# The first keys of attention issued beside the end of a feed-forward layer, in a float32 macaron block

## The chip, the cores and the metric

The kernel runs on one core of a Trainium2 chip, in float32. The number that counts is the device time of one execution in microseconds (us), as the median of several runs. The core has five engines that run side by side, each with its own queue in order: PE (matrix products; PEld is its weight load), DVE (vector), ACT (scalar functions), POOL (general, and here the issuer of the indirect gathers) and SP (issues most DMAs). An instruction waits in its queue until the data, or the memory, that it needs is free, and all that stands behind it on that engine waits as well.

## What is computed

Four batches of 512 positions with 512 features go through a feed-forward layer, an attention layer and the same feed-forward layer again, each with a layer norm ahead and a residual around it:

```
x = x + 0.5 * ffn(layernorm(x))
x = x + attention(layernorm(x))
x = x + 0.5 * ffn(layernorm(x))
```

The feed-forward layer has 2048 inner features. Its three weight matrices are read off cubic splines with few control points:

```
inter = silu(x @ gate_w.T) * (x @ up_w.T)
return inter @ down_w.T
```

The attention is a gated delta rule. Of 16 heads each has one query, one key and two values of 128 features; they pass a causal convolution of four taps and a silu:

```
q = rms_norm(q); k = rms_norm(k)
beta = sigmoid(b_gate); g = -exp(A_log) * softplus(a_gate + dt_bias)
S = S * exp(g_t)
delta = (v_t - k_t @ S) * beta_t
S = S + outer(k_t, delta)
o = q_t @ S
```

The outputs are normalised, multiplied by silu(z) and brought back to 512 features.

## The kernel before

**Program.** `ffn(x -> x1, build=True)`, `attention(x1 -> x2)` and `ffn(x2 -> out, build=False)` run one after the other. x1 and x2 are DRAM tiles, one for each batch. On-chip memory and PSUM are handed out by pools on a stack: a pool that is opened after another was closed gets the same addresses, so its first writes wait until the last users of the old tiles are done.

**Feed-forward layer** (L297). The first call (FFN1) builds its weights from the splines during the first batch (`spline_weights`, L632); pw (L412) is a small constant that is set to zero by DVE. `hidden` makes pg and pu for 16 blocks of 128 inner features (L434), ACT takes silu, DVE multiplies (L443), SP writes the block to DRAM (`hid`, L444). `gather` brings the 2048 rows back in another order, 16 indirect DMAs on POOL (L453). `project` multiplies them by the down weights: sums pm (L477) with copies fm, blocks y<-wr (L487), the rest y<-we (L490) and y<-cm (L493). `back` copies y to yg (L499), transposes it (y_pt, L504) and adds it, in 44 small pieces called boxes, to a copy of x (`ffn_xr`, L532); then the batch is stored (L510). `turn_of(b)` interleaves by hand the hidden products of batch b+1 with the projection of batch b and the `back` of batch b-1; what is left over runs at its end, all gathers first, then units of work one after the other. The last batches have no hidden products to lie beside. In this stage the order on all five engines is the order written, SP's among them.

**Attention** (L798). Work is cut in 64 units, (batch, head). The opening loads constants (cst, cw, wba, dtb, nega, nwh), sets `ones`, two `tt` tiles and `nn` to their constants by POOL (L820, L870), then does for batch 0 the layer norm (`begin(0)`: xt loaded at L883, statistics L888, pow on POOL L893, subtraction and product L895, transposes ln_pt L902), the gates (pb L909, then DVE and ACT), sums of decays (pgs, pe: L969, L978), and **eight keys ahead** (LEAD). A key is: load of w_k (L1049, one buffer), four steps of pj<-xnT,w_k (L998, eight matmul records), taps of the convolution (L1006 on ACT, three L1008 on DVE), tanh (L1016), k (L1020), then its 32x32 blocks pkk (L1029), dg, squares and weights (L1034 to L1088), scan and product dd (L1095, L1098). After four keys `invert` works on their blocks (L1109 to L1128) in many short DVE instructions. Then slots: `slot(un)` prepares unit un (q, v; taps again), makes the key of unit un+8, runs the recurrence of un-1 and the output of un-2. The opening and the slots are in an order written by hand on PE, DVE, ACT and POOL, with SP left to the scheduler. Attention's tiles in PSUM: pa has four banks, shared by ln_pt, pb, pgs, pe, pj and pkk in the opening; pi and pq have two each.

**Feed-forward layer again.** The second call (FFN2) loads its weights from DRAM, loads batch 0 (`ffn_x`, L328), takes statistics (L336 to L341), normalises (ln_xn, L356), transposes (ln_pt, L363) and starts with pf (L369).

Of the kernel before, what the change touches and what calls it, by code (L numbers as in the profile page):

```python
# [1 line left out]

# [15 lines left out]
P = 128  # L18
# [244 lines left out]
def tile_macaron(ctx, tc, x, w_qkvz, w_ba, conv_w, dt_bias, a_log, norm_w, w_out, cps, consts, grid, starts, out):  # L263
# [32 lines left out]

    def ffn(src, dst, build):  # L297
        with ExitStack() as st:
            wp = st.enter_context(tc.tile_pool(name="ffn_w", bufs=1))
            io = st.enter_context(tc.tile_pool(name="ffn_io", bufs=2))  # L300
            fp = st.enter_context(tc.tile_pool(name="ffn_feat", bufs=2 * NG_F))
            sm = st.enter_context(tc.tile_pool(name="ffn_sm", bufs=2))
            wk = st.enter_context(tc.tile_pool(name="ffn_wk", bufs=2))
            ps = st.enter_context(tc.tile_pool(name="ffn_ps", bufs=2, space=PSUM))
            py = st.enter_context(tc.tile_pool(name="ffn_py", bufs=1, space=PSUM))

# [10 lines left out]
            def tick():  # L317
                clock[0] += 1
                for f in calendar.pop(clock[0], ()):
                    f()  # L320

            def drain():
                while calendar:
                    tick()
# [77 lines left out]
            else:  # L402
                for g in range(NG_F):
                    nc.sync.dma_start(wc[g].rearrange("p m i -> p (m i)"), wg_d[g])
                ft = whole(xt)
            wdp = st.enter_context(tc.tile_pool(name="ffn_wd", bufs=1))
            wr = wdp.tile([P, NB, P], F32, name="wr")
# [8 lines left out]
            if not build:  # L416
                nc.sync.dma_start(wr.rearrange("p c h -> p (c h)"), wr_d)
                nc.sync.dma_start(we, we_d)
                nc.sync.dma_start(cm.rearrange("p c h -> p (c h)"), cm_d)
            ip = st.enter_context(tc.tile_pool(name="ffn_inter", bufs=2))  # L420

            def hidden(b, ft):

                to, box = hid[b % 2], {}

                def gate(k):
                    if build and b == 0:
                        block(k, wr, we, cm)
                    product(k, 0)

                def product(k, m):
                    at = (k % 2) * P
                    pm = box[m] = ps.tile([P, S], F32, name=("pg", "pu")[m], tag="gu")
                    nc.tensor.matmul(pm, wc[k // 2][:, m, at : at + P], ft[k // 2], start=True, stop=True)  # L434
                    if m:
                        pg = box[0]
                        later(1, lambda: finish(k, pg, pm))

                def finish(k, pg, pu):
                    sg = wk.tile([P, S], F32, name="ffn_sg")  # L440
                    nc.scalar.activation(sg, pg, AF.Silu)
                    it = ip.tile([P, S], F32, name="ffn_it", bufs=4)
                    nc.vector.tensor_tensor(it, pu, sg, ALU.mult)  # L443
                    nc.sync.dma_start(to[k * P : (k + 1) * P, :], it)  # L444

                return [f for k in range(NB) for f in (lambda k=k: gate(k), lambda k=k: product(k, 1))]
# [14 lines left out]
            def project(b, nat):  # L461
# [35 lines left out]
                def evict(g):  # L497
                    yg = box["yg", g] = wk.tile([P, S], F32, name="yg", tag="yg", bufs=4)
                    nc.scalar.copy(yg, box["y"][g])  # L499
# [44 lines left out]
            def turn_of(b):  # L544
# [10 lines left out]
                plan["nat"], steps = gather(b + 1)  # L555
                tail, early = plan["tail"], []
                for i in range(4):
                    early += [*tail[i : i + 1], *turns[i : i + 1]]
                early += inter
                lead = 6 * 2 if b >= 0 else len(main)  # L560
                for i, f in enumerate(main):
# [9 lines left out]
                    tick()  # L571
                    n = -(-len(early) // max(1, lead - i)) if i < lead else 0
                    if i >= 2 or not turns:
                        for f in early[:n]:
                            f()
                            tick()
                        early = early[n:]
                    if i >= lead:
# [5 lines left out]
                        units = units[n:]  # L584
                drain()

                for f in steps if b + 1 < B else ():
                    f()
                for f in early + units:
                    f()  # L590
                    tick()
                plan["tail"] = back

            by_hand = lambda: tc.manual_schedule(
                engines={e.engine for e in (nc.tensor, nc.vector, nc.scalar, nc.gpsimd, nc.sync)}
            )
# [4 lines left out]
            if build:  # L601
# [16 lines left out]
                built.close()  # L618
            np_ = st.enter_context(tc.tile_pool(name="ffn_nat", bufs=NB + 4))
            with by_hand():  # L620
                if build:
                    plan["nat"], steps = gather(0)
                    for f in steps:
                        f()
                for b in range(0 if build else -1, B):
                    turn_of(b)
                for f in plan["tail"]:
                    f()
                    tick()
                drain()  # L630

    def spline_weights(st, scratch, wc, ps):  # L632

        sp = st.enter_context(tc.tile_pool(name="spl", bufs=1, side="right"))
        s2 = st.enter_context(tc.tile_pool(name="spl2", bufs=2, side="right"))
        c1 = scratch.enter_context(tc.tile_pool(name="spl_c1", bufs=1))
# [158 lines left out]

    def attention():  # L798
        with ExitStack() as st:
            pool = lambda name, bufs, **k: st.enter_context(tc.tile_pool(name=name, bufs=bufs, **k))  # L800
            ac = pool("at_c", 1)
            sm = pool("at_sm", 2)
            sn = pool("at_sn", LEAD + 3)
            w1 = pool("at_w1", 1)
            w2 = pool("at_w2", 2)
            w3 = pool("at_w3", 3)
            w4 = pool("at_w4", 4)
            wkeys = pool("at_k", LEAD + 2)
            pa = pool("at_pa", 4, space=PSUM)
            pi = pool("at_pi", 2, space=PSUM)  # L810
            pq = pool("at_pq", 2, space=PSUM)

            def bank(p, name, shape):
                return p.tile(shape, F32, name=name, tag="bank")

# [3 lines left out]
            ones = ac.tile([P, P], F32, name="ones")  # L819
            nc.gpsimd.memset(ones, 1.0)  # L820
            gt = cst[:, C_GT : C_GT + P]
# [35 lines left out]
            def due():  # L857
                for f in calendar.pop(clock[0], ()):
                    f()
# [9 lines left out]
            for x_ in (*tts, nn):  # L869
                nc.gpsimd.memset(x_, 0.0)  # L870

# [170 lines left out]
            def keys(b, n, bt, s, dd, slot):  # L1042

                xnT, beta, g, eg, neg = (bt[k] for k in ("xnT", "beta", "g", "eg", "neg"))
                at = n * 6 * DK + DK
# [30 lines left out]
                def weights(ms, rs):  # L1076
# [4 lines left out]
                    w = sn.tile([P, NT, 2], F32, name="w")  # L1081
                    nc.vector.tensor_tensor(w, beta[:, :, n, :], bc(rk2, 2, 2), ALU.mult)
                    nw = sm.tile([P, NT, 2], F32, name="nw")
# [510 lines left out]

            with tc.manual_schedule(engines={e.engine for e in (nc.tensor, nc.vector, nc.scalar, nc.gpsimd)}):
                batches[0], load, turn_x, raw, sums = begin(0)
                for t in range(NT):
                    load(t)
                    drain()
                    turn_x(t)  # L1600
                for f in (raw, sums):
                    f()
                    drain()
                made, first = [], iter(())
                ahead = min(LEAD, N)
                for un in range(ahead):
                    if un == GRP:
                        drain()
                        first = invert(diag[0], inverse[0])
                    made.append(keys_of(un))  # L1610
                    made[un]["load"]()
                    made[un]["decay"]()
                    for f in made[un]["dense"]:
                        f()
                        clock[0] += 1
                        due()
                        for _ in range(2):
                            next(first, None)
                    later(6, made[un]["blocks"])
                    if un in (GRP - 1, ahead - 1):  # L1620
                        drain()
                if ahead == GRP:
                    first = invert(diag[0], inverse[0])
                for _ in first:
                    pass
                for un in range(N + 2):
                    slot(un)
                drain()

    ffn(lambda b: x[b], lambda b: x1[b], True)  # L1630
    attention()
    ffn(lambda b: x2[b], lambda b: out[b], False)


# [30 lines left out]
```

## Time and profile before

The time is 3882.93 us, the median of 3 runs (3880.99 to 3885.04). The profiled execution:

| | |
|---|---|
| time of the profiled execution | 3887.16 us |
| its span (first to last instruction) | 3885.4 us |
| PE busy | 3594.6 us (93%) |
| DVE busy | 2631.4 us (68%) |
| ACT busy | 1463.3 us (38%) |
| POOL busy | 855.7 us (22%) |
| mean granted clock of PE | 0.965 |
| last hidden product of FFN1 (pu, L434) | 342.72 us |
| last transposes y_pt of FFN1 | 402.05 to 403.96 us |
| last py product of attention | ends at 3540 us |

Times in lines of the profile are in us from the start of the span. A line of the timeline gives start, duration, engine, source line, operation, output<-input, shape and count, and in square brackets the idle time of the engine just before and what ended it. "SPq" rows are the issue of DMAs, not their flight. A row of windows gives for one stretch of time each engine's busy time and count, then the granted clock of PE, the DMA engines' busy share and GB/s. In the view of 40 slices each digit is a busy share in tenths.

The stages: FFN1 up to 409 us, attention's opening from there to 551, slots to 3540, FFN2 to the end.

### The profile page before, as it was taken

The numbers are of one execution on the slowest core, as the hardware profiler recorded it, in microseconds if no ns is written. First come the engines' busy times: TensorE is split into PE (matmuls) and PEld (weight loads), VectorE is DVE, ScalarE is ACT, GpSimd is POOL, SyncE is SP. The second block draws the span as 40 slices with busy tenths as digits, with TensorE's granted clock in tenths as the row PEclk, the third lists the DMA queues.
The fourth block names the chain that finished last, engine by engine and source line by source line (L and its number), as shares of the span: only waits on it lengthen the run. The fifth ranks groups of instructions, "written<-read, shape, count | busy, mean of one in ns | idle before, by whom it ended". The sixth has DMA issues, their size and how long they took to land. (4 is left out here: it accounts for less than half of the span.)

```text
span 3885.4 us, 62488 instructions
## 1 busy us (share of the span) xinstructions
PE 3594.6 (93%) x24568; PEld 1975.0 (51%) x24568; DVE 2631.4 (68%) x5927; ACT 1463.3 (38%) x3432; POOL 855.7 (22%) x662
## 2 busy tenths in 40 slices
PE   5998569999999999999999999999999999987998
PEld 2332235555555555555555555555555555553333
DVE  5232387788788878878877887888888777652321
ACT  2221113444444444344444443444444444442221
POOL 2113022222222222222222222222222222120221
PEclk7999679999999999999999999999999999997999
DMA  4435211222222222221222221122122211112452
GB/s 140 149 129 174 84 40 57 68 65 58 63 58 63 60 79 61 64 61 58 63 70 80 61 73 54 58 64 59 58 79 64 71 50 55 50 36 95 150 192 98
DMA packets 303093, 302.25 MB, mean 78 GB/s; under 512 B 96880, under 2 KB 231312, under 8 KB 302224
## 3 DMA queue, kind: packets, MB, share of 16 engines
q1 hardware_dynamic: 292560, 264.70, 21.9%
q0 software_dynamic: 10240, 33.56, 2.8%
q8 instruction: 194, 3.18, 0.3%
q14 instruction: 99, 0.81, 0.1%
HBM read 247.60 MB, written 50.59 MB: 77 GB/s over the span
## 5 line engine op out<-in xcount | busy, mean ns | idle before, releaser
L1008 DVE SCALAR_TENSOR_TENSOR acc<-pj,cw,acc 128x511 f32<-128x511 f32 (+2 forms) x768 | 573.7, 747 | 150.1 <-ACT acc L1006 132.0
L998 PE MATMUL pj<-xnT,w_v 128*128 128x512 f32 x1024 | 521.1, 602 | 0.0
L1461 PE MATMUL py<-w_o,gT 128*128 128x512 f32 x1024 | 514.8, 616 | 0.4
L1313 PE MATMUL pz<-w_z,xnT 128*128 128x512 f32 x1024 | 514.5, 614 | 0.0
L443 DVE TENSOR_TENSOR ffn_it<-pu,ffn_sg 128x512 f32<-128x512 f32 x128 | 88.4, 691 | 363.6 <-PE pu L434 253.4
L998 PE MATMUL pj<-xnT,w_k 128*128 128x512 f32 x512 | 267.3, 631 | 19.5 <-DMA w_k<-in_L_attn_W_qkvz 19.5
L998 PE MATMUL pj<-xnT,w_q 128*128 128x512 f32 x512 | 255.3, 602 | 0.0
L1016 ACT ACTIVATE th<-acc 128x512 f32<-128x512 f32 x256 | 163.0, 637 | 237.7 <-DVE acc L1008 228.8
L1369 ACT ACTIVATE tq<-pks,rqe 128x128 f32<-128x128 f32 x384 | 120.4, 364 | 340.4 <-DVE rq L1210 202.0
L1439 ACT ACTIVATE oo<-oo,orr 128x128 f32<-128x128 f32 x512 | 162.6, 389 | 205.9 <-POOL oo L1434 205.9
L1006 ACT ACTIVATE acc<-pj,cw 128x512 f32<-128x512 f32 x256 | 175.3, 685 | 171.7 <-PE pj L998 170.8
L1461 PEld LDWEIGHTS py<-w_o,gT 128*128 128x128 f32 x1024 | 171.4, 192 | 106.3 <-issue 95.2
L1313 PEld LDWEIGHTS pz<-w_z,xnT 128*128 128x128 f32 x1024 | 169.8, 191 | 99.5 <-issue 88.5
L1039 POOL TENSOR_TENSOR rsq<-msq,phalf 128x4 f32<-128x4 f32 x64 | 64.8, 1013 | 685.2 <-DVE msq L1037 685.2
L1039 POOL TENSOR_TENSOR rsk<-msk,phalf 128x4 f32<-128x4 f32 x64 | 68.1, 1064 | 654.8 <-DVE msk L1037 653.2
L998 PEld LDWEIGHTS pj<-xnT,w_v 128*128 128x128 f32 x1024 | 170.7, 191 | 70.7 <-issue 64.1
L1195 POOL TENSOR_TENSOR ks<-kn,ws 128x1024 f32<-128x1024 f32 x64 | 121.6, 1901 | 378.6 <-DVE ws L1188 353.5
L1020 DVE SCALAR_TENSOR_TENSOR vT<-th,acc 128x512 f32<-128x512 f32 x128 | 184.6, 1443 | 23.3 <-ACT th L1016 23.3
L1427 DVE TENSOR_REDUCE om<-osq 128x4 f32<-128x512 f32 x128 | 87.2, 681 | 139.5 <-ACT osq L1426 139.5
L453 POOL DMA_INDIRECT nat<-hid,idx x128 | 121.8, 951 | 268.3 <-PE y_pt L504 105.1
L1120 DVE TENSOR_TENSOR inv<-inv,inv_tmp 128x30 f32<-128x30 f32 (+14 forms) x480 | 168.7, 351 | 16.5
L1377 PEld LDWEIGHTS pzz<-rr,tt 128*128 128x128 f32 x768 | 115.0, 193 | 113.1 <-issue 54.8
(205 smaller groups left out, 6869.0 us busy)
## 6 DMA issues: line engine op xcount, KB each, us to landing
hid<-ffn_it SPq DMA_DIRECT2D x128, 256.0 KB, 2.0
w_v<-in_L_attn_W_qkvz SPq DMA_DIRECT2D x64, 512.0 KB, 3.5
w_z<-in_L_attn_W_qkvz SPq DMA_DIRECT2D x64, 512.0 KB, 4.8
w_o<-in_L_attn_W_out SPq DMA_DIRECT2D x32, 1024.0 KB, 5.6
ab<-decay_c SPq DMA_DIRECT2D x64, 512.0 KB, 3.7
w_k<-in_L_attn_W_qkvz SPq DMA_DIRECT2D x64, 256.0 KB, 2.8
w_q<-in_L_attn_W_qkvz SPq DMA_DIRECT2D x64, 256.0 KB, 3.4
ad<-decay_b SPq DMA_DIRECT2D x256, 32.0 KB, 2.2
```

What stands on the lines that cost most here:

```text
L453: nc.gpsimd.indirect_dma_start(out=nt, out_offset=None, in_=to[:, :], in_offset=bass.IndirectOffsetOnAxis(ap=idx[:, v : v + 1], axis=0),)
L998: nc.tensor.matmul(pj, w()[:, c, col : col + DK], xnT[:, c, :], start=c == 0, stop=c == NC - 1)
L1006: nc.scalar.activation(acc, pj, AF.Copy, scale=cw[:, ch, 3:4])
L1008: nc.vector.scalar_tensor_tensor(acc[:, d:], pj[:, : S - d], cw[:, ch, 3 - d : 4 - d], acc[:, d:], ALU.mult, ALU.add)
L1016: nc.scalar.activation(th, box["acc"], AF.Tanh)
L1020: nc.vector.scalar_tensor_tensor(dest(), box["th"], 1.0, box["acc"], ALU.add, ALU.mult)
L1039: nc.gpsimd.tensor_tensor(rs, ms, phalf[:, :NT], ALU.pow)
L1120: nc.vector.tensor_tensor(ee[:, j + 1 :, :j], ee[:, j + 1 :, :j], tj, ALU.add)
L1195: nc.gpsimd.tensor_tensor(ks, bc(kn, 2, 2), bc(ws, 3, P), ALU.mult)
L1313: nc.tensor.matmul(pz, xnT[:, c, t * P : (t + 1) * P], pair["wz"][:, c].rearrange("p j k -> p (j k)"), start=c == 0, stop=c == NC - 1,)
L1439: nc.scalar.activation(s["oo"][:, t, r], s["oo"][:, t, r], AF.Copy, scale=s["orr"][:, u : u + 1])
L1461: nc.tensor.matmul(box["py"], pair["gT"][r][:, t, :], pair["wo"][:, r, :], start=r == 0, stop=r == 3)
```

## The change

Four things are altered.

- **ffn in two sides.** Its pools are opened in two stacks, `early` (weights lag and wc, x, features, statistics, sg and it, and a new PSUM pool `ffn_gu` of two banks for pg and pu) and `late`, at the other end of memory (`side="right"`: the down weights, yg, ffn_xr, gathered rows, two PSUM banks for pm and transposes, four for y). `early` is closed after the last hidden product has been issued. The spline pools move from right to left.
- **Leftovers with a partner.** `turn_of` returns its leftovers instead of running them; `run` issues one gather, one unit and one step of an iterator `beside` by turns. After `early` is closed, SP is no longer in the written order.
- **attention is a generator.** Its first part yields after each tick, and is driven by FFN1's last `run` calls; at `yield None` it stops until FFN1's pools are closed. In the first part it has two PSUM banks of its own: one for ln_pt, pb, pgs, pe and pj together, one for pkk. Pools w1 and w2 are split in a front part (opened at once) and a back part (opened after `yield None`).
- **Opening in another order.** x rows are loaded two ahead; a key's `decay` is issued with the next key, its `blocks` two keys later; the inversion starts after key 5. `ones`, `tt` and `nn` are set by DVE.

```diff
-    def ffn(src, dst, build):
+    def ffn(src, dst, build, beside=iter(())):
         with ExitStack() as st:
...
+            early, late = (st.enter_context(ExitStack()) for _ in range(2))
+            pool = lambda of, name, bufs, **k: of.enter_context(tc.tile_pool(name=name, bufs=bufs, **k))
...
+            wk = pool(early, "ffn_wk", 2)
+            gu = pool(early, "ffn_gu", 2, space=PSUM)
+            ps = pool(late, "ffn_ps", 2, space=PSUM, side="right")
+            py = pool(late, "ffn_py", 1, space=PSUM, side="right")
...
-                for f in steps if b + 1 < B else ():
-                    f()
-                for f in early + units:
-                    f()
-                    tick()
                 plan["tail"] = back
+                return early_ + units, steps if b + 1 < B else []
+
+            def run(units, steps, beside=iter(())):
+                while units or steps:
+                    for f in steps[:1]:
+                        f()
+                    for f in units[:1]:
+                        f()
+                        tick()
+                    next(beside, None)
+                    units, steps = units[1:], steps[1:]
...
-                for b in range(0 if build else -1, B):
-                    turn_of(b)
-                for f in plan["tail"]:
-                    f()
-                    tick()
+                    left = [], steps
+                for b in range(0 if build else -1, B - 1):
+                    run(*left)
+                    left = turn_of(b)
+
+            early.close()
+            with by_hand():
+                also = beside if B > 2 else iter(())
+                run(*left, also)
+                run(*turn_of(B - 1), also)
+                run(plan["tail"], [], also)
                 drain()
+                for step in beside:
+                    if step is None:
+                        break
...
-            nc.gpsimd.memset(ones, 1.0)
+            nc.vector.memset(ones, 1.0)
...
-                nc.gpsimd.memset(x_, 0.0)
+                nc.vector.memset(x_, 0.0)
...
+            batches[0], load, turn_x, raw, sums = begin(0)
+            load(0)
+            load(1)
+            yield from ticks(9)
+            turn_x(0)
+            load(2)
+            yield from ticks(2)
+            turn_x(1)
+            load(3)
+            yield from ticks(8)
+            turn_x(2)
+            yield from ticks(2)
+            turn_x(3)
+            yield from ticks(1)
+            raw()
+            yield from ticks(1)
+            ahead = min(LEAD, N)
+            made, first = [], None
+            for un in range(ahead + 2):
+
+                if un < ahead:
                     made.append(keys_of(un))
                     made[un]["load"]()
...
+                if un >= 2:
+                    made[un - 2]["blocks"]()
+                for i in range(7):
+                    if un < ahead and i < NC:
+                        made[un]["dense"][i]()
+                    if un == 1 and i == 4:
+                        sums()
+                    if 1 <= un <= ahead and i == 5:
+                        made[un - 1]["decay"]()
+                    yield from ticks(1)
+                    for _ in range(2):
+                        next(first or iter(()), None)
+                if un == GRP + 1:
                     first = invert(diag[0], inverse[0])
+            drain()
+            for _ in first:
+                pass
+            yield None
+            first_banks.close()
+            for f in backs:
+                f()
+            w3 = pool("at_w3", 3)
+            w4 = pool("at_w4", 4)
+            pa = pool("at_pa", 4, space=PSUM)
...
-    ffn(lambda b: x[b], lambda b: x1[b], True)
-    attention()
+    steps = attention()
+    ffn(lambda b: x[b], lambda b: x1[b], True, steps)
+    for _ in steps:
+        pass
     ffn(lambda b: x2[b], lambda b: out[b], False)
```

## The prediction

> **What bounds the kernel now.** I read the 40 slices first, then 20-us windows, then the timeline wherever PE falls.
>
> ```profile
> PE   5998569999999999999999999999999999987998
> DVE  5232387788788878878877887888888777652321
> PEclk7999679999999999999999999999999999997999
> ```
>
> A slice is 97 us. PE is full except at the start, in slices 5 and 6 (388 to 583 us), and near 3500. The slots between are PE's own and the change leaves their instructions and buffers alone, so a gain must come from the dips. The windows of the first (time, PE, PEld, DVE, ACT, POOL, clock, DMA share, GB/s):
>
> ```profile
> 400.00:420.00 20.00, 3.96 (x22) 2.47 (x20) 6.41 (x44) 2.02 (x4) 0.00 (x0) 0.70 0.70 233
> 420.00:440.00 20.00, 11.15 (x48) 9.79 (x48) 6.12 (x16) 2.55 (x5) 2.21 (x4) 0.50 0.27 83
> ...
> 500.00:520.00 20.00, 13.20 (x50) 5.22 (x51) 18.72 (x46) 2.64 (x4) 1.01 (x1) 0.74 0.10 28
> 520.00:540.00 20.00, 9.15 (x107) 4.11 (x106) 18.10 (x58) 1.95 (x3) 5.58 (x6) 0.60 0.14 28
> ...
> 560.00:580.00 20.00, 20.00 (x191) 11.09 (x192) 14.32 (x35) 7.08 (x14) 4.53 (x4) 0.96 0.13 40
> ```
>
> To 480 no engine is full and the clock is down: a chain of waits. From 496 to 551 DVE is full. The timeline gives the chain's ends:
>
> ```profile
> 371.60 0.95 POOL L453 DMA_INDIRECT nat<-hid,idx  x1 [0.30 <-issue]
> ...
> 417.23 0.81 SPq L883 DMA_DIRECT2D xt<-x  x2
> ...
> 420.65 0.69 DVE L888 BATCH_NORM_STATS2 at_st<-xt 128x6 f32<-128x512 f32 x1 [11.56 <-DMA xt<-x]
> ...
> 466.72 3.75 PE L998 MATMUL pj<-xnT,w_k 128*128 128x512 f32 x4 [3.00 <-DMA w_k<-in_L_attn_W_qkvz]
> ...
> 551.53 2.26 DVE L1008 SCALAR_TENSOR_TENSOR acc<-pj,cw,acc 128x511 f32<-128x511 f32 x3
> ```
>
> FFN1's gathers end at 372.5, its PE work at 404, its scatter (boxes, L532) at 409; only at 417 does attention load its x, though batch 0 of x1 was long written. Eight keys follow, some 10 us each (ACT starts them at 454.5, 463.75, ... 525.11), and w_q's taps start at 551.53: until then DVE still works on key 7 and the inversion. Second dip, where FFN2 waits for a load:
>
> ```profile
> 3544.95 0.92 SPq L328 DMA_DIRECT2D ffn_x<-x  x2
> ...
> 3551.00 1.29 DVE L336 BATCH_NORM_STATS2 ln_st<-ffn_x 128x6 f32<-128x512 f32 x2 [10.31 <-DMA ffn_x<-x]
> ```
>
> **The change, part by part.** I track when w_q's taps start: 551.53 now.
>
> *Build.* pw's memset (0.11) stood before copy_predicated on DVE and waited 4.09 for POOL's cfTd. It is now DVE's first instruction; pu, at 61.66 after 1.73 of PE idle, and wg_d and rw behind it come up to 3 earlier. What is late next is DMA rw. Ends 0 and 3.5; I take 3, as that chain has no other wait above 1.
>
> *FFN1's end, later.* POOL's queue now holds, in order, 3 gathers, the pow of x rows 0 and 1 (L893), 9 gathers, pow 2, 2 gathers, pow 3, 2 gathers. A pow waits for DVE's statistics, hence for xt. xt is issued behind nwh (352.54); by the row of 417.23 it lands 3.4 later, some 357. Ahead of the statistics DVE must do nwh (357.2) and the moved memsets. Two of 128x1024 and nn took POOL 2.37. DVE shows only small ones (128x64 in 0.11); ends 0.8 by that and 2.4 by POOL's rows; I take 2.3. nwh's 0.15 and 2.3 of memsets reach 359.7; statistics (0.69 + 0.18 + 0.15) end near 360.8, two pows (0.57) follow, and gather 4 starts near 362 (before: 356.6). Nine at 1.25 end at 373.5, pow 2 is ready; pow 3 needs row 3 (loaded after row 1's transposes), about 377; the last gather ends near 379.6 (before: 372.5). boxes(2), 6.44, stands behind norm 3 on DVE (377.7), ends 384.2; blocks(0) on PE waits for it. It ran from 377.36 once gathers allowed: PE's main stretch starts at 384.5, **7 late**. Behind it are keys' matmuls: everything waits, so these 7 count. Ends 3 (xt lands early) and 14 (its 256 KB rows among gathers; the DMA share of 404 to 417 was 0.89).
>
> Here a rule weighs against the change. The Trainium skill, "SBUF — State Buffer", section "Who interferes with whom" and the box on SWDGE, says that while DVE runs a two-port form GpSimd is locked out and can't write the descriptors of its DMAs. Beside the gathers now come three memsets and four xt TENSOR_SCALARs (0.55): at worst 2.3 + 2.2 = 4.5 more of gather delay. The row: gathers kept 0.94 to 0.95 and 0.30 between through nwh's and nega's TENSOR_SCALARs at 357.19 and 358.59 and 44 boxes, but those are small or another form. I take 0, and 4.5 for the range's end (14 includes it).
>
> *PE's stretch from 384.5.* Blocks 14.2 (2.86 + 10.58 and the gap), pm 2.1, we 3.70, cm 7.03, y_pt 1.9, pb 6.93, keys 0 to 4 at 8 matmuls, pgs and pe 2.9, three pkk at 0.46: the sum without keys is 40.1. For a key, the clock decides.
>
> ```profile
> 490.96 6.49 PE L998 MATMUL pj<-xnT,w_k 128*128 128x512 f32 x8
> ```
>
> The Trainium skill, "TensorE: Matmul & The Clock Gate", Part 1, says that PE falls to half rate after an idle window of about 3.4 us and returns after as long a busy one. This row ran after 5.80 of idle at half rate (0.81 a matmul); cm's 16 in 7.03 (0.44) were at full rate. Inside a busy stretch a key is 3.5 (5 make 17.2), by the idle tail's row 6.5 (32.5). By the rule keys 0 to 4 stay warm, since FFN work lies between; I take 17.2. w_k has one buffer, and a load cost 3.0 of PE idle: here y's blocks and cm lie between, at nothing. If that cover goes, 5 x 3 = 15 returns. All first-part tiles share one PSUM bank, where four were: pgs must wait until taps of key 1 read pj (0.69 + 2.31), pe for eg (0.5): 3.4. Sum 60.7: key 4 is multiplied by **445.2**; with its start on ACT, taps start at 447 (before: 500.76).
>
> *Tail, DVE's.* From 447 DVE owes: taps(4) 2.31, boxes(3)'s rest 3.1 of 6.41, ee scan 2.24, taps and k of keys 5 to 7 (3 x 3.0), six wed scans and dd (1.11 each) 6.7, k(4) 0.69, five dg groups 3.75, five irk groups 3.2, the inversion's multiplications and adds (L1114, L1120) 20.6, its transposes 1.97 + 1.99 + 1.93, and the next inversion's first transpose 1.86, each by its row of 440 to 552. That is **59.3**. Waits among these: w_k on one buffer, pkk in a single bank (pkk of un+1 can't start before dd of un reads it; two were in flight), POOL's pow 1.38 between, keys 5 to 7 at half clock (3 more each, mostly beside the inversion). In 500 to 540 the row of DVE shows 36.8 of 40, so 8% waits; on 59 that is 5, and I take 6.2. Sum: w_q's taps at **512.5**, 39 earlier. Ends: 40 of PE delay and double waits give 530 (gain 22); all waits hidden and PE 7 earlier give 500 (52). POOL's work there (pow, wed, ee 1.90) is light. ACT keeps one table load.
>
> *Slots.* Same instructions and same waits in order; buffers are split to other addresses, which costs 0. No row shows otherwise; ends 0 and plus 4 for the first slot, whose w_q, w_v, w_z loads now come earlier and are only better covered.
>
> *FFN2.* Its ffn_x lies on memory apart from xa. x2 of batch 0 is loaded once ACT and POOL let go of oo, about 3524, behind no x write. Its statistics fit beside the xa adds (2.74 free between). ln_xn needs only the store of x (3540.72, memory handed on by 3544.95) instead of load plus statistics; it started at 3555.38. Now 3545: **10.4**. Ends 4 (the load is behind 3.91 of wc issues and w_o) and 13.
>
> Sum against the profiled execution (span 3885.4, 1.76 around it, 3887.16): 3 + 39 + 10.4 = 52.4 less, some 2 lost to contention of FFN1's last stores with w_k loads (from the 0.89 DMA share), so **50**: 3837. The runs' median, 3882.93, is 4.2 below the profiled run, so **3833**.
>
> **Rivals.**
>
> 1. *Partly hidden* (0.22). Gathers and pows form a chain through DVE and POOL, PE idles and is at half clock: 14 late, keys at 6.5 (15 more), tail waits 12. Opening gains 12 to 18, with 13 elsewhere: about 3855. For it: POOL in order, one bank. Against: PE has 14 of blocks to run from.
> 2. *Packs better* (0.17). xt lands before nwh, gathers lose 3, inversion fits in DVE's gaps while PE multiplies: 500, gain 52 plus 13: 3818. For it: DVE had 9.10 of 61 busy in 343 to 404. The floor: PE's work from 343 to 537 is about 98 us, so at most 94.
> 3. *It does not overlap* (0.04): were xt held by FFN memory as before, only FFN2 and build gain: 13, 3870. The order on PE (key multiplications ahead of y_pt) is against it.
> 4. *Slower* (0.05): each of 64 slots pays for the split buffers or for loads in a different place. Place: w_v's load in a slot, hidden now beside 20.00 of PE in 20. Price: at 0.8 us a slot the gain of 50 is eaten; at 1.0 the time is 3883 - 50 + 64 = 3897. Against: slots keep order and waits, and the DMA share there is 0.13. For it: the tiles that are split (xnT, acc, th, ad, wed) are read in every slot, at other addresses.
>
> **How the numbers follow.** The forecast has 0.52. The range 3810 to 3862 takes in rivals 1 and 2 and leaves out 3, 4 and tails. 0.2% (7.8 us) is about what a measurement here can tell from no change. Faster: 0.52 + 0.22 + 0.17 and most of 3, less a margin for sums of several misses: 0.91; same 0.04; slower 0.05.
>
> **What would show it.** w_q's taps near 512 (not 551) from the start; the first ln_pt before 365; the last gather near 379 and blocks(0) resuming at 384; keys' PE rows at 3.5, not 6.5, up to key 4; PEclk above 0.9 from 385 to 445; in 450 to 510 DVE near 18 of 20; slots at unchanged length; FFN2's first ln_xn about 5 after the last xa add instead of 15. The forecast is wrong if gathers end beyond 386, if pkk's waits spread the tail beyond 525, or if a slot grows.

## The result: 3850.33 us, and the profile after

The changed kernel takes 3850.33 us, the median of 4 runs (3848.84 to 3850.78), against 3882.56 us before (4 runs). The ratio is 0.9916, with a 95% interval of 0.9899 to 0.9933: 32 us faster, where 50 were forecast. The profiled execution of the changed kernel is its median (3850.33, span 3848.6), while that of the kernel before lay 4.6 above its own, so from one profile to the other 36.8 us are to be explained.

The 40 slices of the changed kernel:

```profile
PE   5997768999999999999999999999999999997998
DVE  5232577877888888787788887887888777652321
PEclk8999889999999999999999999999999999997999
```

Against those of before, slice 5 (385 to 481 us) has risen from 5 to 7 tenths for PE and from 3 to 5 for DVE, while PE's 6 in slice 6 has stayed: the dip is shallower, but it is still there. The windows of the dip (time, PE, PEld, DVE, ACT, POOL, clock, DMA share, GB/s) show where:

```profile
400.00:420.00 20.00, 17.31 (x105) 6.12 (x108) 7.34 (x16) 4.58 (x9) 0.10 (x1) 1.00 0.09 26
420.00:440.00 20.00, 19.15 (x127) 7.84 (x120) 7.20 (x21) 1.34 (x3) 3.35 (x5) 1.00 0.22 41
...
480.00:500.00 20.00, 6.45 (x40) 2.79 (x40) 18.68 (x49) 1.95 (x3) 1.64 (x2) 0.77 0.13 32
500.00:520.00 20.00, 1.66 (x65) 1.48 (x66) 15.41 (x43) 0.00 (x0) 3.24 (x4) 0.50 0.09 14
520.00:540.00 20.00, 19.71 (x86) 9.45 (x85) 13.60 (x27) 6.94 (x14) 2.06 (x2) 0.87 0.18 47
```

From 400 to 440, where PE had 15 us of work in 40 before, it has 36 at full clock: keys 0 to 3, and key 4 up to 449.7, run between FFN1's last products, as forecast. But from 480 to 520 PE has 8 us of work in 40 and waits for the end of the opening. The timeline's rows at the places that the prediction named:

```profile
378.04 0.95 POOL L458 DMA_INDIRECT nat<-hid,idx  x1 [0.30 <-DVE ffn_xr L537]
...
450.54 2.31 DVE L1040 SCALAR_TENSOR_TENSOR acc<-pj,cw,acc 128x511 f32<-128x511 f32 x3
...
461.26 0.66 PE L1061 MATMUL pkk<-k 128*32 128x32 f32 x32 [11.11 <-DVE dd L1129]
461.84 6.25 PE L1030 MATMUL pj<-xnT,w_k 128*128 128x512 f32 x8
...
519.65 6.34 PE L1030 MATMUL pj<-xnT,w_q 128*128 128x512 f32 x8 [4.90 <-DVE dd L1129]
...
526.75 2.32 DVE L1040 SCALAR_TENSOR_TENSOR acc<-pj,cw,acc 128x511 f32<-128x511 f32 x3 [5.40 <-ACT acc L1038]
...
3519.65 1.46 DVE L361 TENSOR_SCALAR ln_xn<-ffn_x,ln_mv,ln_rstd 128x512 f32<-128x512 f32 x3 [5.59 <-DMA pw<-in_grid]
```

In order: the last gather ends at 379.0 (379.6 forecast), key 4's taps start at 450.5 (447), and the first w_q taps at 526.75 (512.5 forecast; 551.53 before). The forecast's times leave the build's gain out and the measured ones have it in them; the section on the prediction puts them on one footing. The last row is FFN2's start. The load that it names (pw) was issued 0.5 us behind the store of x, and the row can't tell which of the two ln_xn needed.

The 36.8 us divide as follows. "Base" is the start of the last run of y<-wr products of batch 2, right behind FFN1's last hidden product; slot 2 is taken at its first ACT instruction, because w_q's taps still understate what slots 0 and 1 owe.

| stretch | before | after | gain |
|---|---|---|---|
| start to base (the build) | 343.25 | 341.24 | 2.0 |
| base to slot 2 (the opening) | 292.7 | 266.4 | 26.3 |
| slot 2 to the end of the last xa add | 2904.8 | 2903.4 | 1.4 |
| last xa add to FFN2's first ln_xn | 14.7 | 8.6 | 6.1 |
| from there to the end | 330.0 | 328.9 | 1.1 |

### The profile page after: what moved, and what is told of

Same layout as the page of the kernel before. It is cut to its first block, busy times and chain, and to the rows that moved or that the text cites. A ratio compares the mean times of both kernels' runs of the same rounds, so it can differ in the third digit from the quotient of the medians.

```text
span 3848.6 us, 62481 instructions
## 1 busy us (share of the span) xinstructions
PE 3584.5 (93%) x24568; PEld 1970.3 (51%) x24568; DVE 2633.1 (68%) x5931; ACT 1461.8 (38%) x3432; POOL 851.7 (22%) x658
## 4 chain that ended last, share of the span: by engine, by line
PE 43%; DVE 36%; ACT 8%; POOL 6%; issue 3%; DMA 3%; SPq 1%; DVEq 0%; POOLq 0%; ACTq 0%
DVE acc L1040 13%; PE py L1492 7%; PE pz L1344 6%; DVE vT L1052 4%; PE pj L1030 4%; PE y L492 3%; POOL oo L1465 3%; DVE ee L1212 3%; PE pg L439 3%; PE pu L439 3%; PE pks L1383 2%; POOL orr L1464 2%; ACT tq L1400 2%; PE pu L1329 2%; ACT th L1048 2%
## 5 line engine op out<-in xcount | busy, mean ns | idle before, releaser
L1030 PE MATMUL pj<-xnT,w_k 128*128 128x512 f32 x512 | 260.1, 612 | 0.0
L1052 DVE SCALAR_TENSOR_TENSOR vT<-th,acc 128x512 f32<-128x512 f32 x128 | 185.1, 1446 | 22.8 <-ACT th L1048 22.8
```

The lines of the kernel that those rows point to most:

```text
L1030: nc.tensor.matmul(pj, w()[:, c, col : col + DK], xnT[:, c, :], start=c == 0, stop=c == NC - 1)
L1052: nc.vector.scalar_tensor_tensor(dest(), box["th"], 1.0, box["acc"], ALU.add, ALU.mult)
```

## The experiments

The runs were made in three batches, and a batch could fall on another chip: the kernel before took 3933.71, 3930.56 and 3883.89 us in them. So times are compared as ratios within a batch (1 us is 0.00026), and traces by the stretch from base to slot 2, in which the changed kernel differed by 1.6 us between two batches.

| run | time | ratio to before, 95% interval | base to slot 2 |
|---|---|---|---|
| changed kernel, first result | 3850.33 | 0.9916 (0.9899 to 0.9933) | 266.4 |
| changed kernel, second batch | 3896.36 | 0.9918 (0.9901 to 0.9934) | 268.0 |
| e1 four pkk in the bank | 3902.13 | 0.9917 (0.9900 to 0.9934) | 266.8 |
| e2 pkk behind the product | 3907.66 | 0.9932 (0.9916 to 0.9949) | 269.7 |
| e3 no partner | 3903.95 | 0.9921 (0.9904 to 0.9938) | 263.1 |
| e4 FFN2's weights late | 3900.28 | 0.9911 (0.9894 to 0.9927) | 268.2 |
| e5 one inversion step a tick | 3891.05 | 0.9897 (0.9881 to 0.9914) | 263.4 |
| e6 slots' banks first | 3890.03 | 0.9898 (0.9881 to 0.9914) | 259.0 |
| e7 e5 and e6 | 3888.97 | 0.9894 (0.9877 to 0.9910) | 258.3 |
| e8 norm held until FFN1's end | 3870.47 | 0.9963 (0.9948 to 0.9977) | 287.4 |
| e9 gathers first | 3852.61 | 0.9920 (0.9903 to 0.9936) | 267.2 |
| e10 e4, e5 and e6 | 3841.74 | 0.9887 (0.9870 to 0.9903) | 262.9 |
| e11 e3, e4 and e6 | 3840.80 | 0.9888 (0.9872 to 0.9905) | 260.1 |

One part of that stretch varies by itself. In the runs with a partner PE stands idle for 2.1 us between key 1's product and pgs. In the second batch's run of the changed kernel, and in e1, e4, e5 and e10, the granted clock fell there, and key 2 reached ACT 90.6 to 91.8 after base. In the first result, e2, e6 and e7 it stayed, and key 2 came at 87.0 to 87.9 (in e9, too, it stayed, but every key was late). The same kernel did both (ten us around pgs, second batch and first result):

```profile
431.58:441.58 10.00, 8.30 (x68) 4.24 (x68) 2.46 (x6) 1.59 (x3) 0.21 (x2) 0.66 0.06 14
```

```profile
416.24:426.24 10.00, 8.88 (x85) 3.76 (x85) 2.69 (x10) 1.60 (x3) 1.82 (x4) 1.00 0.08 15
```

So a stretch is best compared with one in which the clock did the same.

**Is it the single bank of pkk?** The trace after shows PE waiting 11.11 us for dd before a pkk, with the next key's product queued behind it. Two edits aim at that.

```diff
+            four = []
...
+                if p is None and name == "pkk":
+                    if not four:
+                        t4 = pf.tile([P, 4, *shape[1:]], F32, name=name, tag="kk")
+                        four.extend(t4[:, k] for k in range(4))
+                    return four.pop(0)
                 if p is None:
-                    return pf.tile(shape, F32, name=name, tag="kk" if name == "pkk" else "bank")
+                    return pf.tile(shape, F32, name=name, tag="bank")
```

> Four keys' pkk (512 bytes a partition each) lie side by side in the one bank, so pkk of a key no longer waits for dd of the key before. Theory A (in PE's queue the wait of pkk for dd holds the next key's multiplication, and that is where the tail lost its time): PE's 11.11 us of idle before pkk at 461.26 and 4.28 at 472.37 go, key 5's multiplication starts near 453 instead of 461.8, DVE's idle between 450 and 527 falls from 20.6 to about 10, w_q's taps start near 517 instead of 526.75, time 3839 to 3843. Rival B (DVE's in-order queue and the half clock set the tail, the bank only shows up in it): less than 3 us, 3848 to 3850.

Nothing changed: 0.9917, and the wait is still in the trace.

```profile
481.62 0.40 DVE L1135 TENSOR_TENSOR dd<-pkk,wed 128x256 f32<-128x256 f32 x1
...
482.07 0.65 PE L1067 MATMUL pkk<-k 128*32 128x32 f32 x32 [10.04 <-DVE dd L1135]
482.65 5.84 PE L1036 MATMUL pj<-xnT,w_k 128*128 128x512 f32 x8
```

pkk starts right behind the other key's dd although it writes another quarter of the bank. So e1 did not take away the wait that it meant to, and tells nothing on theory A. The second edit leaves the wait and takes the product out from behind it:

```diff
-                if un >= 2:
-                    made[un - 2]["blocks"]()
                 for i in range(7):
+                    if un >= 2 and i == 4:
+                        made[un - 2]["blocks"]()
...
-                if un == GRP + 1:
-                    first = invert(diag[0], inverse[0])
+                    if un == GRP + 2 and i == 3:
+                        first = invert(diag[0], inverse[0])
```

> The single bank stays, but a key's pkk is issued behind the next product instead of ahead of it; the first inversion starts half a key later for it. Theory A in its form 'PE's order, not the bank's size': the product no longer stands behind the wait, key 5's multiplication starts near 453, gain 5 to 9 us, 3841 to 3845. If the bank's size alone counts (dd to pkk to dg to pow to dd is a chain of its own, about 6 us a key): gain under 3, 3847 to 3851. Rival B: no change, or 1 to 3 slower by the later inversion.

Key 5 reached ACT 119.4 after base instead of 126.9 and key 7 at 146.6 instead of 151.2; yet slot 2 came at 269.7, later than without the edit. PE's wait was real, and this edit, which also starts the inversion half a key later, got nothing out of freeing it. So theory A falls in the form that PE's order alone costs the time. In its other form, that only one pkk can be in flight, it stands untested: the expectation gave that form under 3 us for this edit, and no run here gave pkk a second bank.

**Is it the overlap at all?** FFN1 runs to its end without `beside`; the first part of attention is driven behind it, and since it then lies outside the hand-ordered stretch, the scheduler places it.

```diff
-    ffn(lambda b: x[b], lambda b: x1[b], True, steps)
+    ffn(lambda b: x[b], lambda b: x1[b], True)
     for _ in steps:
         pass
```

> The changed kernel with FFN1 run to its end without a partner, and attention's first part behind it; everything else of the change stays. If the overlap carries the opening's gain and build and FFN2's start the rest (2.0, 6.0 and 1.1 by the traces), it takes 3873 to 3876, or more if the opening's new form (one bank, later blocks) is slower by itself: then 3878 to 3890. If the gain came from elsewhere than the overlap: 3850 to 3860.

The main expectation was wrong and the last of its three branches came: 0.9921, equal to the changed kernel (its four runs spread over 8 us). Its timeline says why:

```profile
371.54 29.00 SPq L915 DMA_DIRECT2D xt<-x  x4
...
438.14 3.67 PE L1030 MATMUL pj<-xnT,w_k 128*128 128x512 f32 x8 [0.88 <-ACT beta L952]
...
535.81 6.47 PE L1030 MATMUL pj<-xnT,w_q 128*128 128x512 f32 x8 [5.71 <-DVE dd L1129]
537.60 0.09 DVE L1153 MEMSET inv<- 128x32 f32 x1
538.36 1.93 DVE L1157 STREAM_TRANSPOSE rt<-inv 128x1024 f32<-128x1024 f32 x1
540.14 2.00 DVE L1159 STREAM_TRANSPOSE rn<-inv 128x1024 f32<-128x1024 f32 x1
...
544.08 2.27 DVE L1040 SCALAR_TENSOR_TENSOR acc<-pj,cw,acc 128x511 f32<-128x511 f32 x3
```

With memory free for it, the scheduler itself put the norm's loads and statistics at FFN1's end (xt issued 9 us after base, as in the changed kernel). The first key starts only behind FFN1's last product, 79.2 after base instead of 61.2. All of that and more is made up later: from key 4's start on ACT to w_q's taps it takes 52.1 us (491.97 to 544.08) where the changed kernel takes 77.0 (449.74 to 526.75). The rows at the end show the difference: here w_q's product runs while DVE ends the inversion and its transposes; in the changed kernel DVE had one transpose (1.92) to do beside it and then waited 5.40. Two things differ between these kernels, where the keys lie and who orders them; a run with the keys behind FFN1 in the written order was not made.

**What is the early opening worth?** e8 is e3 with the norm kept from starting early: it reads batch 3 of x1, which is stored last.

```diff
-                    nc.sync.dma_start(xt, x1[b][t * P : (t + 1) * P, :])
+                    nc.sync.dma_start(xt, x1[b or B - 1][t * P : (t + 1) * P, :])
```

> As the run without a partner, but the first part's layer norm reads batch 3 of x1 in place of batch 0 (the attention of batch 0 is then computed from the wrong rows), so that it can't start before FFN1's last store. Theory D (what the change hides is the opening's chain of loads, norm and gates; the keys' products beside FFN1 only wait longer afterwards): the first key starts 18 to 27 us later against FFN1's last hidden product than in the run without a partner, and the time is 18 to 27 us longer than that run's, 0.9965 to 0.9990 of the kernel before. Rival (the opening's other order alone carries the gain): it stays within 6 us of the run without a partner, 0.992 to 0.994.

```profile
411.20 9.41 SPq L915 DMA_DIRECT2D xt<-x  x4
414.42 0.69 DVE L920 BATCH_NORM_STATS2 at_st<-xt 128x6 f32<-128x512 f32 x1 [10.97 <-DMA xt<-x]
...
435.74 6.44 PE L1030 MATMUL pj<-xnT,w_k 128*128 128x512 f32 x8 [0.88 <-ACT beta L952]
```

The first key comes 105.3 after base, slot 2 at 287.4: 24.3 later than in e3, and only 5 ahead of the kernel before. By ratios it is 0.0042, 16 us, a little under the 18 to 27 expected; the spread of e3's runs covers part of that gap. Theory D holds: what the change hides is the chain load, statistics, pow, transposes, pb. That the loads had waited for memory which FFN1 held, and that the split gives it, is read off the pools and the times of issue (417.23 in the kernel before, 9 us after base here); no run tests the split alone.

**What sets the end of the tail?** Two edits on the changed kernel, alone and together, beside the changed kernel itself.

> The changed kernel once more, as the yardstick of this batch of runs: 0.990 to 0.993 of the kernel before.

```diff
                     yield from ticks(1)
-                    for _ in range(2):
-                        next(first or iter(()), None)
+                    next(first or iter(()), None)
```

> The first inversion goes on by one step a tick instead of two, so that its instructions stand less often ahead of the keys' taps, scans and dd on DVE, and its last steps and transposes come behind dd of key 7. Theory C (the tail is a chain key to pkk to pow to dd, and the written order of DVE puts inversion pieces ahead of its links; DVE is half idle from 507.75 to 526.75): dd of key 7 comes 8 to 12 us earlier, the rest of the inversion lies beside w_q's multiplication, 5 to 9 us faster than the changed kernel. Theory A (the single pkk bank): 0 to 2 faster. Theory B (DVE is simply full, 55.6 us of work): no change.

```diff
-            pa = pool("at_pa", 4, space=PSUM)
             pi = pool("at_pi", 2, space=PSUM)
             pq = pool("at_pq", 2, space=PSUM)
+            pa = pool("at_pa", 4, space=PSUM)
```

> pi and pq are opened ahead of pa, so that pa's four banks are not the ones that pkk held and w_q's multiplication need not wait for dd of key 7 (4.90 us of PE idle and then 6.34 + 0.69 us in which DVE waited 5.40). Theory C: 4 to 7 us faster than the changed kernel. If DVE's chain only shifts (the recurrence or pp then waits for pi's banks): 0 to 2.

> One step a tick and the slots' banks together. With dd of key 7 early, w_q's product is early too, and what is left of the inversion is then DVE's last work: the two gains overlap. 7 to 12 us faster than the changed kernel if both waits were real, as much as the better one alone if they are the same wait.

Against the changed kernel in the same batch (3896.36) they give 5.3, 6.3 and 7.4 us, and base to slot 2 shrinks by 4.6, 9.0 and 9.7. The intervals of the ratios overlap, but every run of e6 and e7 is below every one of the changed kernel's. Part of the 9.0 and 9.7 is the clock ahead of pgs: against the first result, in which it also stayed up, they are 7.4 and 8.1. The times are in the ranges that theory C gave (dd of key 7 came 6.2 earlier against base in e5, where 8 to 12 were expected), and together the edits give little more than e6 alone: it is nearly the same wait, seen from two sides. e5's rows (first two) have dd of key 7 before the inversion's end (533.2) and w_q's taps 8.4 behind it; e6's (last three) have one transpose (1.90) and no wait between the last dd and the taps, whose product was long done:

```profile
530.11 0.42 DVE L1129 TENSOR_TENSOR dd<-pkk,wed 128x256 f32<-128x256 f32 x1
...
538.95 2.29 DVE L1040 SCALAR_TENSOR_TENSOR acc<-pj,cw,acc 128x511 f32<-128x511 f32 x3
```

```profile
504.66 1.27 ACT L1038 ACTIVATE acc<-pj,cw 128x512 f32<-128x512 f32 x2 [9.62 <-PE pj L1030]
...
531.48 0.42 DVE L1129 TENSOR_TENSOR dd<-pkk,wed 128x256 f32<-128x256 f32 x1
533.77 2.27 DVE L1040 SCALAR_TENSOR_TENSOR acc<-pj,cw,acc 128x511 f32<-128x511 f32 x3
```

The x2 in e6's ACT row are key 7 and w_q, one behind the other.

**Do the gathers' 7 us count?** e9 issues all gathers of a batch before the interleaved units.

```diff
+                for f in steps:
+                    f()
+                steps = []
                 while units or steps:
-                    for f in steps[:1]:
-                        f()
```

> The changed kernel with all gathers of a batch issued ahead of the interleaved units, so that no pow stands between batch 3's gathers in POOL's queue. If the 7 us that the gathers lost count for everything behind them: the last gather ends some 8 us earlier, the time is 4 to 7 us below the changed kernel (0.990). If the layer norm, which now stands behind the gathers, or the tail's chain takes it back: within 2 us of the changed kernel (0.9915 to 0.992), or slower.

The last gather started at 368.34 instead of 378.04, and the time did not move (0.9920). The pows now stood behind the gathers: the last row of xt was normalised at 379.64 instead of 376.60, and boxes(2), behind it on DVE, started at 380.10 instead of 377.12. What was 7 late in the forecast can be put on the gathers or on the norm, but it is not saved by changing their order.

**FFN2's start.** e4 takes wr, we and cm (1.8 MB of loads) out of the moment in which the last batch of x is stored, and loads them some products later.

```diff
-            if not build:
-                nc.sync.dma_start(wr.rearrange("p c h -> p (c h)"), wr_d)
...
                 for i, f in enumerate(main):
+                    if b < 0 and i == 8:
+                        nc.sync.dma_start(wr.rearrange("p c h -> p (c h)"), wr_d)
...
```

> FFN2's wr, we and cm (1.8 MB) are loaded some products later instead of beside the store of x. If these loads slow the store (ln_xn started 8.6 us behind the last xa add; in the kernel before the store let memory go 4.2 us after its issue), ln_xn starts 4.5 to 5.5 behind the add and the time is 3846 to 3848. If ln_xn waits for something else: 3850, unchanged.

```profile
3532.56 0.69 DVE L1495 TENSOR_TENSOR xa<-py,xa 128x512 f32<-128x512 f32 x1 [2.74 <-PE py L1492]
...
3537.90 1.46 DVE L361 TENSOR_SCALAR ln_xn<-ffn_x,ln_mv,ln_rstd 128x512 f32<-128x512 f32 x3 [1.62 <-DMA pw<-in_grid]
```

From the end of the last add to ln_xn it is now 4.65 us instead of 8.63, as expected; in time it is 0.0005 against the first result, 2 us, which is inside the intervals, so that the gain is shown by the trace alone. The row still names pw's load, so that the edit shows what the 1.8 MB beside the store and this load cost, and not which of the two ln_xn needs.

**A faster version.** The parts were put together, on the changed kernel and on e3.

> One inversion step a tick, the slots' banks, and FFN2's down weights later, all in one. The parts lie at different places of the time: 7.4 (both) and about 3 add up, 10 us below the changed kernel, 0.989 of the kernel before.

> FFN1 without a partner, attention's first part behind it in the scheduler's order, with the slots' banks and FFN2's late down weights. w_q's product waited 5.71 us for dd of key 7 there too, but beside it DVE had inversion and transposes to do: 1 to 4 from the banks and 3 from the weights, 0.990 to 0.991. If order by hand is what the overlap needs, it is slower than e10 by 4 or more; if not, equal.

Both are 42 to 43 us faster than the kernel before and some 10 faster than the change, and equal to each other. (e10's stretch is 4.6 longer than e7's; key 2 came 3.4 later in it, with the clock down ahead of pgs.) So in two pairs (e3 and the changed kernel, e11 and e10) the keys' products beside FFN1 brought nothing that could be measured over keys behind FFN1 in the scheduler's order.

## Why the prediction was right in sign and too large

The forecast was 3833 with 50 us of gain; measured, 3850.33 with 32. The time lies in the range of 3810 to 3862. The forecast's times behind the build are on the base of the kernel before (343.25), and the measured base came 2.0 earlier, so each step is measured from base here; the gain of the opening to w_q's taps was 22.8 and not 39. Step by step:

- **Build**: 3 forecast, 2.0 measured. The mechanism was right (pw's memset no longer stands before copy_predicated).
- **FFN1's end**: the last gather, 379.6, ended at 379.0, and boxes(2), 384.2, at 383.5: both 1.4 later than forecast from base. The chain of pow, norm and boxes was followed right. The moved memsets took 0.91, 0.91 and 0.48 (2.3 forecast, 2.3 measured).
- **The SBUF rule**: three gathers after a pow, beside an xt TENSOR_SCALAR, took 0.99 to 1.00 instead of 0.95. The 4.5 us of the rule's reading did not come; 0 was right. No gather ran beside the memsets, so these stay untried.
- **PE's stretch and the clock rule**: keys 0 to 3 ran at a granted clock of 1.00 between 400 and 440, keys 5 to 7 near half rate (6.25, 5.81 and 5.86 for eight). Key 4's taps came at 450.5 for 447, from base 5.5 after the forecast.
- **The tail**: this is the step that failed. The prediction had 59.3 of DVE work and "I take 6.2" for waits. From 450.54 to 526.75 the windows of the changed kernel give, and PE's row of key 7's pkk:

```profile
450.54:526.75 76.21, 28.09 (x195) 12.69 (x196) 55.64 (x157) 5.27 (x8) 8.74 (x11) 0.64 0.32 96
...
475.76:507.75 31.99, 10.11 (x78) 4.31 (x76) 29.25 (x86) 2.63 (x4) 3.27 (x4) 0.71 0.11 25
507.75:526.75 19.00, 7.76 (x43) 3.64 (x44) 9.62 (x21) 0.69 (x1) 2.24 (x3) 0.55 0.09 15
```

```profile
514.09 0.66 PE L1061 MATMUL pkk<-k 128*32 128x32 f32 x32 [10.82 <-DVE dd L1129]
```

  The work was 55.6, less than forecast; the waits were 20.6 instead of 6.2. With key 4's lateness and the smaller work that is 5.5 + 14.4 - 3.7 = 16.2, the whole of the miss (526.75 - 512.5 and the base's 2.0: 16.3). The 8% of waits had been read off a stretch of the kernel before (500 to 540) in which DVE was hardly ever short of work: the inversion went on to 533, and w_q's product ran from 537.2, ahead of the last dd (543.4). Of the 20.6, 8.5 lie before 475.76, among keys 3 to 5, 2.7 in the middle and 9.4 at the end. In the new order the inversion is done at 507.75, the dd of keys 6 and 7 are still to come, one link after the other, and w_q's product stands behind the last of them: DVE is busy 9.6 of the last 19. The prediction did see pkk's single bank, but looked for its price among the keys, where freeing PE (e2) was worth nothing; a price that could be saved was at the end, where the slots' first bank was the one that key 7's pkk held (e6). That and the inversion's pace (e5) are worth 5 to 7 us of time. The rest of the extra waits no run removes: pkk of key 7, whose k was ready at 505.65, waited for dd of key 6 until 514.09, and how much of that is the one bank's and how much the written order's stays open.
- **FFN2**: 10.4 forecast, 6.1 measured. The load and the statistics are off the path, as forecast; one term was not right: the store's 4.2 us came from the kernel before, where wr, we and cm had been issued 8 to 10 us ahead of it. Here they are issued beside it (e4).
- **Slots**: 0 forecast for their addresses and 1.4 faster measured; the slower rival's 0.8 us a slot is excluded.
- **The rivals**: the time lies nearer to "partly hidden" (3855) than to the forecast, but not by all of its means: PE was neither 14 late nor at half rate for keys 0 to 4; only its longer waits in the tail came true. "It does not overlap" was priced at 3870 for xt held until FFN1's end. That case is e8, and the price was right: 0.9963 is 3868 beside the 3882.56 of the first batch. What e3 does not bear out is that the rest needs the keys' overlap: it lets no key overlap and has all of the gain.
- **Luck**: in the profiles the tail, FFN2 and the build fell short by 16.3, 4.3 and 1.0. Against that, 8.4 us came from terms that had been put at nothing or below: slots 0 and 1 (3.5), the other slots (1.4), the rest of FFN2 (1.1) and 2.4 taken off for contention. That they narrowed the miss to 13.2 is luck. The other 4 us of the 17 lie in the kernel before, whose profiled execution was slower than its median.

## What to carry to other kernels

When a serial stretch is moved beside other work, ask first which part of it is waiting and which is working: here the loads, statistics and pows were the waits, and moving them alone brought the opening's gain. A sum of an engine's work plus a share of waits holds only where that engine has other work ready; where the last links form a chain, price the chain link by link to the instruction that starts the next stage. Look also at which buffer that instruction takes, since a pool opened over a released one hands on the last reader's wait.

## What the runs showed of the hardware that had not been expected

A long busy stretch did not by itself bring the clock back. pb's 32 small matmuls (128x64, each with its own weight load) took 7.09 us, and PE was busy all of the eight us around them at half clock (first row). In e3 the same 32 took 3.79, behind cm and y_pt at full rate (second row):

```profile
386.00:394.00 8.00, 8.00 (x40) 6.70 (x39) 0.43 (x2) 0.75 (x3) 0.00 (x0) 0.50 0.16 59
```

```profile
433.48 3.79 PE L941 MATMUL pb<-wba,xnT 128*128 128x64 f32 x32 [0.67 <-ACT xnT L935]
```

So it mattered what ran before them, and these short matmuls did not lift the clock. By the clock rule on which the prediction leaned, so long a busy stretch would have; here the measurement decides. The rule's idle window did not fit either: in five runs the clock fell at the idle of 2.1 us ahead of pgs or just behind it, and in five others, with the same idle, it did not.

The same program differed between batches, which may be chips, almost only in the feed-forward layers. The changed kernel took 3850.33 in one and 3896.36 in another (profiled executions 3850.33 and 3893.81); from slot 2 to the last add both took 2903.4, but base came at 341.24 and 356.58, and from FFN2's first ln_xn to the end it was 328.9 and 355.2. In the slower one PE stood idle before pf for up to 11.1 us, with nothing in the profile that it waited for; the cause stays open.
